# First attention stage: the causal penalty preset in the scores' banks, and P's transposes placed right behind the scores

## The chip, the cores and the metric

The kernel runs on one core of a Trainium2 chip. The metric is the device time of one execution in microseconds (us). It is a single launch that computes two blocks of a small transformer on an input of 4 sequences of 512 tokens with 128 features each, all in 32-bit floats.

## The reference, cut to what matters

The whole is `x = x + attention(layernorm(x))`, then `x = x + six local attention and feed-forward layers(layernorm(x))`. The change lies in the first half alone. That half is an ordinary causal attention with 16 heads of 64 features, whose mask is not minus infinity but a finite penalty of -50:

```python
q = (x @ Wq).reshape(b, s, HEADS, HEAD_DIM)      # k and v alike
scores = SCALE * jnp.einsum('bqhd,bkhd->bhqk', q, k)
causal = jnp.triu(jnp.ones((s, s), dtype=x.dtype), k=1)
scores = scores + MASK_PENALTY * causal
attn = jax.nn.softmax(scores, axis=-1)
out = jnp.einsum('bhqk,bkhd->bqhd', attn, v).reshape(b, s, HEADS * HEAD_DIM)
return out @ Wr
```

Because the penalty is finite, all keys count for every query, and all 512 columns of the scores are computed.

## The kernel before, in words

The order of the work is written out by hand: each engine executes its instructions in the order in which the program issues them, and semaphores tell an engine that something it reads is there, or that a buffer it writes is free.

**Slots.** The first stage has 64 slots, numbered m = 0 to 63. There are 4 sequences (`b`), 8 pairs of heads each (`c`), and 4 row tiles of 128 queries each (`t`). A slot does two row tiles of one pair of heads: an even slot tiles 0 and 1, an odd slot tiles 2 and 3. An object of the class `Rows` is one row tile; `now` are the two of this slot, `old` the two of the slot before.

**What a row tile goes through.**

- `scores` (line 308): q times k for both heads into `ps_sc`, two banks of PSUM, 512 columns per head. The two heads lie in the two halves of the array's rows and run side by side. 4 products of 256 columns; a 32-bit product is 2 instructions of TensorE, so a row tile is 8 records.
- `penalty` (line 323): for each head, one 16-bit product of an identity with the 128x128 triangle `pen` adds -50 above the diagonal in the tile's own block of columns. The blocks to the right of it get their -50 through a second bias (line 339) of the exponents.
- `maximum` (VectorE, line 335): the row maxima of both heads, over 1024 columns.
- `exponents` (ScalarE, line 348): 4 instructions: for each head the seen columns, and for each head the columns right of them with the other bias. The last tile has 2, of 512 columns. Each also sums its row into `den`.
- `inverse` (VectorE, lines 358 and 359), `normalise` (GpSimd, line 362): the exponents times 1/`den`.
- `transposes` (TensorE, line 373), one slot later: 4 transposes per head into a bank `ps_pt`. ScalarE copies head 0's bank to SBUF (line 377), VectorE head 1's (line 381). There are two such banks, so each group of 4 transposes waits until the group two before it has been copied out.
- `times_v1` (line 393), four slots later, 4 products of 512 columns per slot; after the second half VectorE copies the result out (line 403).

**What else is in a slot.** An even slot projects the next pair's q (line 271, copied by ScalarE, line 273), an odd one its k (line 277, copied by VectorE, line 279). Odd slots also project a part of v (line 287, copied by ScalarE, line 294; the first two slots two parts more), but for the last four odd slots of the last sequence. All these go through one single bank `ps_pj`: the next product into it waits for the copy of the one before. Some even slots hold a step of a layernorm, in the same bank: a mean (line 109, then VectorE line 111 and a square on ScalarE, line 113), a variance (line 118, then an inverse root of 12 small GpSimd instructions, lines 81 to 84), and a scaling (line 126, then VectorE line 130). The odd slots with c = 1 of the later three sequences end with the output projection of the sequence before (line 407, 8 products of 512 columns), again in that bank.

**The order in a slot, before.** TensorE: `times_v1`, scores of both tiles, penalties of both tiles, v or a layernorm step, transposes of `old[0]`, q or k, transposes of `old[1]`, output projection. ScalarE: v's copy or the square, head 0's copy of `old[0]`, the exponents of `now[0]`, those of `now[1]`, q's copy, head 0's copy of `old[1]`. VectorE: the copy of line 403, a scaling step, the maximum of `now[0]`, mean or variance, bias, head 1's copy of `old[0]`, maximum and bias of `now[1]`, k's copy, `inverse` of `now[0]`, head 1's copy of `old[1]`, `inverse` of `now[1]`.

After the first stage come the six local layers with their own loop of slots; their code is unchanged.

Of the kernel before, what the change touches and what calls it, by code (L numbers as in the profile page):

```python
# [8 lines left out]
F32 = mybir.dt.float32  # L9
# [6 lines left out]
P = 128  # L16
# [16 lines left out]
def body(ctx: ExitStack, tc: tile.TileContext, a, out: bass.AP):  # L33
# [156 lines left out]
    with tc.manual_schedule():  # L190
# [2 lines left out]
        wv = s1.tile([P, INNER], F32, tag="wv", name="wv")  # L193
        wr = s1c.tile([P, NC, EMB], F32, tag="wr", name="wr")
        pen = s1.tile([P, P], BF16, tag="pen", name="pen")
        xr = [s1.tile([P, NT, EMB], F32, tag="xr", name=f"xr{b}", bufs=2) for b in range(B)]
        for b in range(B):
            src = x[b].rearrange("(t p) e -> p t e", p=P)
            if b:
                nc.sync.dma_start(out=xr[b], in_=src)  # L200
            else:
                nc.sync.dma_start(out=xr[b][:, 0:2], in_=src[:, 0:2])
                nc.scalar.dma_start(out=xr[b][:, 2:NT], in_=src[:, 2:NT])
                nc.sync.dma_start(out=ident16, in_=a["ident16"])
                nc.sync.dma_start(out=pen, in_=a["pen"])
        for t_, n_ in ((wq, "wq"), (wk, "wk"), (wv, "wv")):
            nc.scalar.dma_start(out=t_, in_=a[n_])
        nc.sync.dma_start(out=wr, in_=a["wr"].rearrange("(c p) e -> p c e", p=P))
# [87 lines left out]
        class Rows:  # L296


            def __init__(self, b, c, t):
                self.b, self.c, self.t = b, c, t  # L300

            def scores(self):
                b, c, t = self.b, self.c, self.t
                sc = self.sc = ps1.tile([P, 2, S], F32, tag="sc", name="ps_sc", bufs=2)
                for k0 in range(0, S, S // 2):
                    for h in range(2):
                        rows = slice(h * HD, (h + 1) * HD)
                        mm(  # L308
                            sc[:, h, k0 : k0 + S // 2],
                            lhsT=qs[b, c][rows, t * P : (t + 1) * P],  # L310
                            rhs=ks[b, c][rows, k0 : k0 + S // 2],
                            start=(k0 == 0),
                            stop=False,
                            skip_group_check=True,
                        )

# [24 lines left out]
            def exponents(self):  # L341
                self.pr = s1.tile([P, 2, S], F32, tag="pr1", name="pr1", bufs=3)
                self.den = small.tile([P, 2, 2], F32, tag="den", name="den")
                seen = (self.t + 1) * P
                for part_, cols in enumerate((slice(0, seen), slice(seen, S))):
                    for h in range(2):
                        if cols.start < S:
                            nc.scalar.activation(  # L348
                                self.pr[:, h, cols],
                                self.sc[:, h, cols],  # L350
                                AF.Exp,
                                bias=self.nm[:, part_, h : h + 1],
                                accum_out=self.den[:, part_, h : h + 1],
                            )

            def inverse(self):
                if self.t + 1 < NT:
# [26 lines left out]
        def times_v1(b, c, half):  # L384

            if half == 0:
                os_[b, c] = ps1b.tile([P, S], F32, tag="o1", name="ps_o1", bufs=1)
            o = os_[b, c]
            for k in (2 * half, 2 * half + 1):
                for h in range(2):  # L390
                    col = (2 * c + h) % HEADS * HD
                    j, col = col // 512, col % 512
                    mm(  # L393
                        o[h * HD : (h + 1) * HD, :],
                        lhsT=vs[b, j][:, k, col : col + HD],
                        rhs=pTs[b, c][:, h, k, :],
                        start=(k == 0),
                        stop=(k == NT - 1),
                        skip_group_check=True,
                    )  # L400
# [21 lines left out]
        for m in range(last):  # L422
# [2 lines left out]
            old = rows[2 * m - 2 : 2 * m] if m else []  # L425
            if m >= 4:
                g = m // 2 - 2
                times_v1(g // NC, g % NC, odd)
# [7 lines left out]
            scale = None  # L436
            if not odd and c == 3 and b + 1 < B:
                scale = norms[b + 1][2]
            if b in range(1, B) and not odd and c == 6:
                scale = norms1[b - 1][2]  # L440
            if scale:
                scale()
# [9 lines left out]
            if not odd and 1 <= c <= 2 and b + 1 < B:  # L452
                if c == 1:
                    norms[b + 1] = norm_x(b + 1)
                norms[b + 1][c - 1]()
            if b in range(1, B) and not odd and 4 <= c <= 5:
                norms1[b - 1][c - 4]()
            if now:
                now[0].bias()
# [21 lines left out]
            if now:  # L481
                now[1].exponents()
            for f in copies:
                f()
            if now:
                now[1].inverse()
                now[1].normalise()
            if out_:
# [399 lines left out]
    def first_slot():  # L888
# [8 lines left out]
        rows[-1].transposes(later=True)()  # L897
        first_step()
        square(new, 0)
        times_v1(B - 1, NC - 2, 1)  # L900
        rotate(new, 0)
        sum_squares(new, 0)
        add_rotated(new, 0)
# [8 lines left out]
        times_v1(B - 1, NC - 1, 1)  # L912
        second_step()
        over_norm(new, 0)
        over_norm(new, 1)
# [188 lines left out]
def _constants(n):  # L1104
# [42 lines left out]
    return {"tabs": tabs, "band": band, "pen": pen, "ident16": ident16, "zeros": zeros}  # L1147


# [49 lines left out]
```

## Time and profile before

| | |
|---|---|
| time, median of 3 runs (lowest, highest) | 2072.2 us (2071.69, 2074.13) |
| the profiled execution's own time | 2072.4 us |
| its span | 2070.6 us |
| mean granted TensorE clock | 0.996 |
| first scores start / last slot's scores start | 23.5 us / 523.2 us |
| busy in 130 to 200 us: TensorE, VectorE, ScalarE, GpSimd | 69.99, 46.58, 43.67, 32.76 of 70 us |

The span is what the profiler saw between the first and the last instruction; the rest of the execution's time, 1.8 us, lies around it. "PE" is TensorE's products, "PEld" its loads of weights, DVE is VectorE, ACT ScalarE, POOL GpSimd, SP the queue that issues most transfers. A line of the timeline gives start, length, engine, source line, operation, what it writes from what, and in brackets how long the engine had been idle and what ended that. The chain of waits walks back from the last instruction to whatever released each one; its pieces are lengths of time that add up.

### The profile page before, as it was taken

Reading aid. Unit: us, or ns where it says so; the run is one execution under the profiler, and the core shown is the slowest. Engines: PE = TensorE matmul, PEld = TensorE weight load, DVE = VectorE, ACT = ScalarE, POOL = GpSimd, SP = SyncE. Lnnn points to the kernel's source line nnn. Section 1 sums busy time; section 2 is a strip of 40 time slices with the busy share of each in tenths; the row PEclk is TensorE's granted clock in tenths of the full one; section 3 lists DMA queues with packets and bytes.
Section 4 is the critical chain, followed back from the end, with each engine's and each line's share of the span. In section 5 each row is a group of like instructions: output and inputs, shape, how many; then the busy total and the mean of one; then the engine's idle time right before and its main releaser. Section 6 shows DMA issues by size and latency. Waiting matters only on the chain.

```text
span 2070.6 us, 77263 instructions
## 1 busy us (share of the span) xinstructions
PE 2028.4 (98%) x34382; PEld 1329.1 (64%) x34382; DVE 1640.8 (79%) x2240; ACT 1368.2 (66%) x2678; POOL 1316.5 (64%) x1432
## 2 busy tenths in 40 slices
PE   7999999999999999999999999999999999999998
PEld 5665555655466666666666666666666666666665
DVE  3766766767698888888888888888888888888885
ACT  3665665666455766676776676776667776677763
POOL 1554554555677677667767667667677767667762
PEclk8999999999999999999999999999999999999999
DMA  3000000000011121111211112111121111211110
GB/s 127 1 1 1 1 1 1 1 1 1 12 44 36 42 67 44 44 44 33 77 44 34 54 36 64 53 35 44 46 64 44 38 51 46 67 41 44 38 45 27
DMA packets 34968, 77.44 MB, mean 37 GB/s; under 512 B 4686, under 2 KB 18764, under 8 KB 34636
## 3 DMA queue, kind: packets, MB, share of 16 engines
q1 hardware_dynamic: 33932, 70.79, 11.8%
q8 instruction: 272, 4.46, 0.9%
q10 hardware_dynamic: 704, 1.70, 0.2%
q14 instruction: 60, 0.49, 0.1%
HBM read 23.50 MB, written 1.05 MB: 12 GB/s over the span
## 4 chain that ended last, share of the span: by engine, by line
PE 91%; DVE 5%; ACT 2%; POOL 1%; issue 1%; DMA 0%; SPq 0%; POOLq 0%; ACTq 0%
PE ps_proj L548 23%; PE ps_one L661 12%; PE ps_one L762 7%; PE ps_att L737 7%; PE ps_sc L308 6%; PE ps_o L393 6%; PE ps_att L700 5%; PE ps_pt L373 5%; PE ps_proj L812 3%; PE ps_proj L813 3%; PE ps_proj L832 3%; PE ps_pj L287 1%; PE ps_att L690 1%; PE ps_pj L277 1%; PE ps_pj L271 1%; PE ps_pj L407 1%
## 5 line engine op out<-in xcount | busy, mean ns | idle before, releaser
L587 POOL TENSOR_TENSOR rot<-rot,t 128x1024 f32<-128x1024 f32 x192 | 454.2, 2366 | 232.6 <-DVE t L576 220.1
L548 PE MATMUL ps_proj<-wqkv,xs 128*128 128x512 f32 x1152 | 569.0, 602 | 0.5 <-PE ps_one L661 0.2
L362 POOL TENSOR_TENSOR pr<-pr,den 128x1024 f32<-128x1024 f32 x128 | 241.0, 1893 | 248.3 <-DVE den L359 238.5
L606 POOL TENSOR_TENSOR rot<-rot,ss 128x1024 f32<-128x1024 f32 x192 | 361.3, 1903 | 7.4
L560 ACT ACTIVATE sq<-ps_proj 128x1024 f32<-128x1024 f32 x192 | 196.4, 1023 | 93.8 <-PE ps_proj L548 93.6
L548 PEld LDWEIGHTS ps_proj<-wqkv,xs 128*128 128x128 f32 x1152 | 188.2, 190 | 102.0 <-issue 92.1
L570 DVE TENSOR_TENSOR rot<-ps_proj,lt 128x1024 f32<-128x1024 f32 x192 | 233.3, 1215 | 10.2 <-ACT sq L560 10.0
L576 DVE TENSOR_TENSOR t<-ps_proj,lt 128x1024 f32<-128x1024 f32 x192 | 232.9, 1213 | 0.0
L348 ACT ACTIVATE pr<-ps_sc,nm 128x128 f32<-128x128 f32 (+3 forms) x448 | 220.3, 509 | 11.8 <-DVE nm L335 8.6
L565 DVE TENSOR_REDUCE ss<-sq 128x16 f32<-128x1024 f32 x192 | 221.1, 1190 | 0.0
L661 PEld LDWEIGHTS ps_one<-ident,rot 128*128 128x128 f32 x1536 | 172.7, 141 | 61.2 <-issue 51.2
L661 PE MATMUL ps_one<-ident,rot 128*128 128x128 f32 x1536 | 205.1, 276 | 1.1 <-POOL xs L170 0.6
L335 DVE TENSOR_REDUCE nm<-ps_sc 128x2 f32<-128x1024 f32 x128 | 155.9, 1218 | 62.9 <-PE ps_sc L323 62.8
L664 ACT COPY pT<-ps_one 128x512 f32<-128x512 f32 x192 | 110.0, 587 | 136.6 <-PE ps_one L661 136.6
L762 PEld LDWEIGHTS ps_one<-aT,wo 128*128 128x128 f32 x1536 | 182.9, 192 | 23.6 <-issue 17.7
L762 PE MATMUL ps_one<-aT,wo 128*128 128x128 f32 x1536 | 189.1, 276 | 0.3 <-ACT tmp_t L852 0.2
L746 DVE RECIPROCAL rden<-ps_att 128x8 f32<-128x8 f32 x192 | 38.8, 202 | 176.8 <-PE ps_att L737 176.7
L648 ACT COPY vt<-ps_proj 128x512 f32<-128x512 f32 x192 | 103.1, 590 | 96.4 <-PE ps_proj L548 96.4
L373 PEld LDWEIGHTS ps_pt<-ident,pr 128*128 128x128 f32 x1024 | 117.4, 142 | 58.5 <-issue 47.4
L664 ACT COPY qT<-ps_one 128x512 f32<-128x512 f32 x192 | 103.1, 589 | 66.1 <-PE ps_one L661 66.1
L377 ACT COPY pT<-ps_pt 128x512 f32<-128x512 f32 x128 | 75.6, 591 | 98.0 <-PE ps_pt L373 98.0
L373 PE MATMUL ps_pt<-ident,pr 128*128 128x128 f32 x1024 | 135.9, 274 | 3.0 <-DVE pT L381 2.4
(178 smaller groups left out, 3763.2 us busy)
## 6 DMA issues: line engine op xcount, KB each, us to landing
vs<-vt SPq DMA_DIRECT2D x96, 390.0 KB, 3.7
vs<-vt SPq DMA_DIRECT2D x72, 130.0 KB, 3.6
wqkv<-in_wqkv_dram SPq DMA_DIRECT2D x18, 512.0 KB, 4.0
vs<-in_zeros_dram SPq DMA_DIRECT2D x24, 130.0 KB, 3.7
wo<-in_wo_dram SPq DMA_DIRECT2D x6, 512.0 KB, 4.2
w<-in_w_dram SPq DMA_DIRECT2D x6, 341.0 KB, 5.9
xr<-in_x_dram SPq DMA_DIRECT2D x3, 256.0 KB, 7.6
scales<-in_scales_dram SPq DMA_DIRECT2D x6, 128.0 KB, 3.1
```

What stands on the lines that cost most here:

```text
L348: nc.scalar.activation(self.pr[:, h, cols], self.sc[:, h, cols], AF.Exp, bias=self.nm[:, part_, h : h + 1], accum_out=self.den[:, part_, h ...
L362: nc.gpsimd.tensor_tensor(self.pr, self.pr, self.den[:, 0].unsqueeze(2).to_broadcast([P, 2, S]), ALU.mult)
L373: nc.tensor.transpose(pt[:, k * P : (k + 1) * P], self.pr[:, h, k * P : (k + 1) * P], ident)
L548: mm(p[:, c, :], lhsT=u.xs[:, u.T * P : (u.T + 1) * P], rhs=wpart[j][:, c * 512 : (c + 1) * 512], start=True, stop=True,)
L565: nc.vector.tensor_reduce(u.ss[:, j * HEADS : (j + 1) * HEADS], heads(u.sq[j]), AX.X, ALU.add)
L570: nc.vector.tensor_tensor(heads(t0), heads(pf), lt[:, u.T, 2 * j].unsqueeze(1).to_broadcast([P, HEADS, HD]), ALU.mult)
L576: nc.vector.tensor_tensor(t1.rearrange("p (h t d) -> p h t d", t=2, d=half), pf.rearrange("p (h t d) -> p h t d", t=2, d=half)[:, :, ::-1, :],
L587: nc.gpsimd.tensor_tensor(u.r[j], u.r[j], u.t1, ALU.add)
L606: nc.gpsimd.tensor_tensor(heads(u.r[j]), heads(u.r[j]), u.ss[:, j * HEADS : (j + 1) * HEADS].unsqueeze(2).to_broadcast([P, HEADS, HD]), AL ...
L661: nc.tensor.transpose(tp[:, c * P : (c + 1) * P], src[:, (4 * g + c) * P : (4 * g + c + 1) * P], ident)
L664: nc.scalar.copy(dst[:, 4 * g : 4 * g + 4, col0 : col0 + P], tp.rearrange("p (c t) -> p c t", c=4))
L762: mm(y[:, 0:P], lhsT=wo_w[0][:, k, :], rhs=u.aT[:, g].rearrange("p (j f) -> p j f", f=P)[:, :, f0 : f0 + W], start=(k == 0), stop=(k == NC ...
```

## The change

The penalty products are left out in all slots but the first. In their place ScalarE copies a 32-bit triangle `pen32` (one more small input) for both heads into the tile's own block of `ps_sc`, before the scores, and the scores are added to it. For that the scores of a head are cut into three products: the own block of 128 columns (added to what stands there), the far pair of blocks with 256 columns, and the neighbour block with 128. The preset for the same bank in the next slot stands on ScalarE behind the last exponents that read the bank.

The order in a slot is another one too. TensorE: `times_v1`, scores, transposes of `old[0]`, v or a layernorm step, transposes of `old[1]`, q or k, output projection. ScalarE: head 0's copy of `old[0]`, the seen exponents of `now[0]`, v's copy or the square, the other exponents of `now[0]`, the preset for the next slot's first tile, the exponents of `now[1]`, the preset for its second tile, head 0's copy of `old[1]`, q's copy. VectorE: maximum and bias of `now[0]`, the copy of line 403, head 1's copy of `old[0]`, the layernorm steps (scaling now in the same place as the others), maximum and bias of `now[1]`, head 1's copy of `old[1]`, k's copy, both `inverse`.

```diff
+        pen32 = s1.tile([P, P], F32, tag="pen32", name="pen32")
...
                 nc.sync.dma_start(out=pen, in_=a["pen"])
+                nc.sync.dma_start(out=pen32, in_=a["pen32"])
...
+            def preset(self):
+                sc = self.sc = ps1.tile([P, 2, S], F32, tag="sc", name="ps_sc", bufs=2)
+                nc.scalar.copy(
+                    sc[:, :, self.t * P : (self.t + 1) * P], pen32.unsqueeze(1).to_broadcast([P, 2, P])
+                )
...
             def scores(self):
                 b, c, t = self.b, self.c, self.t
-                sc = self.sc = ps1.tile([P, 2, S], F32, tag="sc", name="ps_sc", bufs=2)
-                for k0 in range(0, S, S // 2):
+                own = self.sc is not None
+                if not own:
+                    self.sc = ps1.tile([P, 2, S], F32, tag="sc", name="ps_sc", bufs=2)
+                sc, far = self.sc, (1 - t // 2) * 2
+                for k, (k0, n) in enumerate(((t, 1), (far, 2), (t ^ 1, 1))):
+                    cols = slice(k0 * P, (k0 + n) * P)
                     for h in range(2):
                         rows = slice(h * HD, (h + 1) * HD)
                         mm(
-                            sc[:, h, k0 : k0 + S // 2],
+                            sc[:, h, cols],
                             lhsT=qs[b, c][rows, t * P : (t + 1) * P],
-                            rhs=ks[b, c][rows, k0 : k0 + S // 2],
-                            start=(k0 == 0),
-                            stop=False,
+                            rhs=ks[b, c][rows, cols],
+                            start=(k == own),
+                            stop=own or k == 2,
                             skip_group_check=True,
                         )
...
-                nc.vector.tensor_copy(at, o)
+                return lambda: nc.vector.tensor_copy(at, o)
...
             for r in now:
                 r.scores()
-            for r in now:
+            for r in now if m == 0 else ():
                 r.penalty()
...
-            if now:
-                now[0].maximum()
+            now[0].maximum()
+            now[0].bias()
+            if m >= 4:
+                keep()
+            if old:
+                old[0].transposes()
+            now[0].exponents((0,))
             if m < 2:
                 make_v(0, 0, 2 * m)
                 make_v(0, 0, 2 * m + 1)
...
-            if old:
-                old[0].transposes()
-            out_ = b > 0 and c == 1 and odd
-            if now:
-                now[0].exponents()
-                if not out_:
-                    now[1].maximum()
-                    now[1].bias()
+            now[0].exponents((1,))
+            if m + 1 < last:
+                rows[2 * m + 2].preset()
+            now[1].maximum()
+            now[1].bias()
+            copies = []
+            if old:
+                copies.append(old[1].transposes(later=True))
             bn, cn = (b, c + 1) if c + 1 < NC else (b + 1, 0)
-            copies = []
             if bn < B:
                 copies.append((make_k if odd else make_q)(bn, cn))
-            if out_ and now:
-                now[1].maximum()
-                now[1].bias()
-            if now:
-                now[0].inverse()
-                now[0].normalise()
-            if old:
-                copies.append(old[1].transposes(later=True))
-            if now:
-                now[1].exponents()
+            now[0].inverse()
+            now[0].normalise()
+            now[1].exponents()
+            if m + 1 < last:
+                rows[2 * m + 3].preset()
             for f in copies:
                 f()
```

More of the change, by code (lines that the diff above doesn't have):

```diff
@@ L299, in __init__ @@
             def __init__(self, b, c, t):
[L300 removed]
+                self.b, self.c, self.t, self.sc = b, c, t, None
+            def preset(self):
[3 more added lines that the diff above has]
+                )
             def scores(self):
                 b, c, t = self.b, self.c, self.t
[L304 to L305 removed]
+                own = self.sc is not None
[4 more added lines that the diff above has]
+                    cols = slice(k0 * P, (k0 + n) * P)
                     for h in range(2):
@@ L339, in bias, with exponents @@
                     nc.vector.tensor_scalar(self.nm[:, 1], self.nm[:, 0], PEN, None, ALU.add)
-            def exponents(self):
-                self.pr = s1.tile([P, 2, S], F32, tag="pr1", name="pr1", bufs=3)
-                self.den = small.tile([P, 2, 2], F32, tag="den", name="den")
+            def exponents(self, parts=(0, 1)):
+                if 0 in parts:
+                    self.start_exponents()
                 seen = (self.t + 1) * P
@@ L346, in exponents @@
                     for h in range(2):
-                        if cols.start < S:
+                        if part_ in parts and cols.start < S:
                             nc.scalar.activation(
@@ L354, in exponents, with start_exponents @@
                             )
+            def start_exponents(self):
+                self.pr = s1.tile([P, 2, S], F32, tag="pr1", name="pr1", bufs=3)
+                self.den = small.tile([P, 2, 2], F32, tag="den", name="den")
             def inverse(self):
@@ L402, in times_v1 @@
                 at = aTs[b, c] = s1c.tile([P, S], F32, tag="aT1", name="aT1", bufs=NC + 2)
-                nc.vector.tensor_copy(at, o)
+                return lambda: nc.vector.tensor_copy(at, o)
+            return lambda: None
         def project_out1(b, y):
@@ L427, in body @@
                 g = m // 2 - 2
-                times_v1(g // NC, g % NC, odd)
+                keep = times_v1(g // NC, g % NC, odd)
             for r in now:
                 r.scores()
-            for r in now:
+            for r in now if m == 0 else ():
                 r.penalty()
@@ L434, in body @@
                 load_x(m)
[L436 to L442, printed above, removed]
-            if now:
-                now[0].maximum()
+            now[0].maximum()
[5 more added lines that the diff above has]
+            now[0].exponents((0,))
             if m < 2:
@@ L451, in body @@
                 make_v(b + 1, 0, c - NT)
-            if not odd and 1 <= c <= 2 and b + 1 < B:
+            if not odd and 1 <= c <= 3 and b + 1 < B:
                 if c == 1:
@@ L455, in body @@
                 norms[b + 1][c - 1]()
-            if b in range(1, B) and not odd and 4 <= c <= 5:
+            if b in range(1, B) and not odd and 4 <= c <= 6:
                 norms1[b - 1][c - 4]()
-            if now:
-                now[0].bias()
-            if old:
-                old[0].transposes()
-            out_ = b > 0 and c == 1 and odd
-            if now:
-                now[0].exponents()
-                if not out_:
-                    now[1].maximum()
-                    now[1].bias()
+            now[0].exponents((1,))
[4 more added lines that the diff above has]
+            copies = []
+            if old:
+                copies.append(old[1].transposes(later=True))
             bn, cn = (b, c + 1) if c + 1 < NC else (b + 1, 0)
-            copies = []
             if bn < B:
                 copies.append((make_k if odd else make_q)(bn, cn))
-            if out_ and now:
-                now[1].maximum()
-                now[1].bias()
-            if now:
-                now[0].inverse()
-                now[0].normalise()
-            if old:
-                copies.append(old[1].transposes(later=True))
-            if now:
-                now[1].exponents()
+            now[0].inverse()
[3 more added lines that the diff above has]
+                rows[2 * m + 3].preset()
             for f in copies:
                 f()
[L485 to L488, printed above, removed]
+            now[1].inverse()
+            now[1].normalise()
+            if b > 0 and c == 1 and odd:
                 y = bank1()
@@ L899, in first_slot @@
         square(new, 0)
-        times_v1(B - 1, NC - 2, 1)
+        times_v1(B - 1, NC - 2, 1)()
         rotate(new, 0)
@@ L911, in first_slot @@
         inverse_norms(new)
-        times_v1(B - 1, NC - 1, 1)
+        times_v1(B - 1, NC - 1, 1)()
         second_step()
@@ L1146, in _constants @@
     zeros = np.zeros((W, 2, NC, HD + 1), f)
-    return {"tabs": tabs, "band": band, "pen": pen, "ident16": ident16, "zeros": zeros}
+    return {"tabs": tabs, "band": band, "pen": pen, "pen32": pen.astype(f), "ident16": ident16, "zeros": zeros}
 def kernel(**inputs):
```

## The prediction, made before the changed kernel had run

> **What bounds the kernel now.** I read the page's head first (engines, then the 40 slices), then the chain of waits in two neighbouring slots, then the timeline of a slot in which transposes already follow transposes.
>
> ```profile
> span 2070.6 us, 77263 instructions
> ...
> PE 2028.4 (98%) x34382; PEld 1329.1 (64%) x34382; DVE 1640.8 (79%) x2240; ACT 1368.2 (66%) x2678; POOL 1316.5 (64%) x1432
> ...
> PE   7999999999999999999999999999999999999998
> ...
> PEclk8999999999999999999999999999999999999999
> ```
>
> TensorE is busy nearly throughout, at full granted clock. The first stage is the first ten slices (scores start at 23.5 us, the last slot's at 523.2).
>
> ```profile
> by line: PE ps_sc L308 37.3%; PE ps_o L393 28.7%; PE ps_pt L373 22.5%; PE ps_pj L271 10.8%; PE ps_sc L323 4.1%
> ...
> 104.33 1.93 PE ps_sc L308 x16
> 106.25 0.33 PE ps_sc L323 x4
> 106.58 0.88 PE ps_pt L373 x8
> 107.46 0.86 PE ps_pj L271 x2
> 108.32 0.92 PE ps_pt L373 x8
> 109.24 1.87 PE ps_o L393 x8
> ```
>
> A plain even slot is TensorE work end to end, with no piece of another engine: 6.78 us from scores to scores. Odd slots add v's product and last 7.72. So whatever leaves TensorE's queue is gained, and whatever it must wait for is lost. Each tr (8 transposes, 0.87 us) now has 0.86 us of other work between it and the next: that is cover, and the change takes it away. What its loss costs is on view in slot 62, the next to last, where no q is left to project and the two groups of transposes follow each other:
>
> ```profile
> 518.57 1.04 PE L373 MATMUL ps_pt<-ident,pr 128*128 128x128 f32 x8
> 518.66 1.22 DVE L335 TENSOR_REDUCE nm<-ps_sc 128x2 f32<-128x1024 f32 x1 [1.80 <-PE ps_sc L323]
> 519.21 0.58 ACT L377 COPY pT<-ps_pt 128x512 f32<-128x512 f32 x1 [2.15 <-PE ps_pt L373]
> ...
> 519.94 0.63 PE L373 MATMUL ps_pt<-ident,pr 128*128 128x128 f32 x4 [0.33 <-POOL pr L362]
> ...
> 519.99 0.68 DVE L381 COPY pT<-ps_pt 128x512 f32<-128x512 f32 x1
> ```
>
> Each half of the second group waits until a copy has emptied its bank. The first half starts 0.15 us after ScalarE's copy ends (519.79), whatever the label names; the second begins at 520.73, 0.06 after VectorE's copy, and its first transpose lasts 0.055 longer than the others (its weights). The next product of another line begins at 521.32, 2.75 us after 518.57, where 16 transposes at 0.109 and a 0.13 change of tile shape make 1.87: 0.88 us lost.
>
> **The change, part by part.** Times count from the first score of a slot (s), and slots from 0.
>
> 1. *Penalties out.* From the first penalty to the next line's first product is 0.23 us (518.33 to 518.57). 63 slots: **-14.5**.
>
> 2. *Scores in three pieces.* The records of line 308 start 0.216 apart in pairs (two heads at once). Per slot 8 such pairs (1.72) become 4 of 256 columns and 8 of 128. A 128-column pair is bounded below by half, 0.108, and above by the pace of weight loads: line 118 (one column, so loads alone) starts 0.1115 apart, and the second head's load goes out 0.007 behind the first's: 0.119. I take 0.112, line 118's pace: 0.86 + 0.90 = 1.76, +0.034 in 64 slots: **+2.2** (0 to +6).
> [...]
>
> 3. *Transposes behind transposes.* The first group starts at s+1.96. Its head 0 is done after 4x0.109 + 0.165 (a transpose lasts 0.273 and the next starts after 0.109) = 0.60, ScalarE copies 0.04 later for 0.585, TensorE's first useful column comes 0.11 after (0.06 + 0.05): 1.34 instead of 0.87, 0.47 lost. Head 1 is done at 1.04; VectorE is free (the maximum now waits for the first tile alone: s+1.2 to 2.4), copies until 1.76, +0.11 = 1.87 against 1.78: 0.09 more. 0.56 per slot in the 12 even slots without a layernorm step and in slots 57 and 61, which have no v: +7.8. Slot 62 has it already and loses less than its 0.88: -0.35. **+7.5**.
>
> 4. *k waits for v's copy* (odd slots). v ends at s+3.70. On ScalarE the copy now stands behind head 0's copy (from s+2.60, the next may start 0.48 later) and two exponents of 384 columns (0.555 each, start to start): s+4.19 to 4.78. k's product goes at 4.89; the second transposes end at 4.57. 0.32 lost, less 0.04 that k's piece shows over q's now. 26 slots with v from slot 5 on: **+7.3**. Before, v's copy was first in the slot.
>
> 5. *Output projection directly behind k*, in the same single bank: k's copy must end first. What such a succession costs: line 287 behind line 287 starts 1.80 us apart at 35.90, for 0.86 of product, 0.94 lost; so far the second transposes covered it. 3 slots: **+2.7**.
>
> 6. *Layernorm steps* stand behind VectorE's copy now. Mean (5 slots): the square starts on ScalarE at s+4.6 and the queue behind it, 0.48 + 2x0.555 + 0.5 for a preset between exponents (their accumulators are read out first) + 4x0.45 + 0.6 to the second preset's end, is through at s+9.05, while the next slot's second tile, which needs that preset, is due at s+8.35: it starts 0.1 later still, 0.75 late after 0.16 today, +0.6 each; q's wait of 0.16 in these slots goes: +2.2. Variance (6 slots): 12 GpSimd operations at 0.285 (3.4 us) start at s+4.6 instead of about 4.0, `normalise` behind them ends at s+9.9, the next first transposes are due at 9.35: 0.75 with the hand-over, and 0.9 once more in slot 59 for the second: +5.4. Scaling (6 slots): bank waits that now cost about 0.7 (slot 22 lasts 7.93 against 6.78 + 0.44) fall to 0.25: -2.7. **+4.9**.
>
> 7. *Presets.* No copy of 128x256 by ScalarE into PSUM stands in the trace. Ends: 0.23 (line 598, 32 columns) and 0.68 (exponent of 512). Nearest: the copy of 512 takes 0.59, and 256 columns fewer are worth 0.20 (exponents 0.68 and 0.48): **0.39**. [...] In plain slots ScalarE's idle time hides two presets (43.67 of 70 us busy; the second ends at s+7.65, the next slot's second tile is due at s+8.0). In slots 0 to 3 TensorE waits for exponents today (the scores' two tiles start 1.82 apart at 31.02 and 32.84), so 8 presets are paid there: **+3.1**. From about 0.55 each on the cover in even slots is gone too. Ends: -2 and +12 us on the whole sum.
>
> 8. *The rest at nothing:* pen32's 64 KB on SP's queue ahead of the later sequences' x (0 to 0.3 us: the first 25 us move 262 GB/s, and x of sequence 1 is needed only in the first normalisation); VectorE and GpSimd do the same work.
>
> Sum: -14.5 + 2.2 + 7.5 + 7.3 + 2.7 + 4.9 + 3.1 = **+13.2**. The profiled execution took 2072.4 (span 2070.6 and 1.8 around it), 0.2 above the median: 2085.6, rounded **2086**.
>
> **Rivals.**
>
> - *The waits stay covered (faster).* TensorE is full, and 14.5 leaves its queue. If copies came early enough that the second transposes find both banks empty and k finds v's copy done, only parts 1, 2, 5 and 7 remain: 2072.4 - 6.5 = 2066. It decides at 0.10 us of new waiting per slot. Against it: two copies of 0.59 and 0.68 cannot fit behind 0.87 us of transposes even on idle engines; slot 62 shows it.
> - *Only the banks cost (no change).* If v's copy and the layernorm steps slip in without delay: parts 1, 2, 3, 5, 7: +1, 2073. For it: ScalarE is idle a third of the time. Against: v's copy is behind exponents in program order.
> - *ScalarE becomes the bound.* A preset of 0.6 to 0.68: +7 to +12 more, 2093 to 2098. For it: even slots have only 0.35 to spare; against: copies run shorter than exponents.
> - *The scores don't get by with less.* If the two heads' loads went one after the other, 128-column pairs would take 0.22: +55, about 2140. Against: the second pair of loads of a slot starts 0.108 behind the first pair, with both heads' products running.
>
> **How the numbers follow.** A difference under 0.2% (4 us) can't be told from none. Chances: forecast 0.68 (its own range 2078 to 2093), ScalarE bound 0.14, only the banks 0.10, covered 0.06, loads in series 0.02. Range 2076 to 2098: it takes in both ends of the preset (-2, +12) and leaves out the faster case and most of the unchanged one. Faster 0.06, the same 0.10, slower 0.84.
>
> **What would show it.** Right: plain even slots of about 7.1 us with an idle of TensorE before the second transposes ended by ScalarE's copy; odd ones of about 7.7 with a wait before k; about 13 us more than today between the first and the last slot's scores (499.7); scores plus hand-over 1.9 instead of 2.16. Wrong: no wait before the second group of transposes; the second tile's scores waiting for presets in plain slots (ScalarE); 128-column records more than 0.12 apart in pairs.

## The result and the profile after

The changed kernel took **2093.9 us** (median of 4 runs, 2092.3 to 2095.2) where the kernel before took 2073.2 beside it (4 runs, 2071.7 to 2076.0): ratio 1.0103, 95% interval 1.0090 to 1.0116, so 1% slower. The prediction was 2086 in a range of 2076 to 2098. The sign came out as predicted, and so did most of the forecast waits; the loss of 21 us is over half as large again as the forecast 13, because of two things for which the prediction has no term. The profiled execution took 2095.2 us.

The head of the page of the kernel after, engines and slices:

```profile
span 2093.5 us, 77885 instructions
...
PE 2030.4 (97%) x34642; PEld 1332.7 (64%) x34642; DVE 1676.2 (80%) x2240; ACT 1418.7 (68%) x2804; POOL 1318.4 (63%) x1432
...
PE   7999999999999999999999999999999999999997
...
PEclk7999999999999999999999999999999999999999
```

TensorE does no less: the span is 22.9 us longer at nearly the same busy time. ScalarE gained 50.5 us, 47.4 of them the presets. VectorE gained 35.4 us, although the change gives it nothing to do. No term of the prediction has that last number; it is the lead to what was missed.

The chain of waits through a plain even slot after (slot 10), the counterpart of the slot shown for before; columns are start, length, what:

```profile
111.77 1.96 PE ps_sc L322 x24
113.73 0.60 PE ps_pt L391 x4
114.33 0.02 issue
114.35 0.59 ACT pT L395
114.95 0.14 issue
115.08 1.11 PE ps_pt L391 x8
116.19 0.86 PE ps_pj L273 x2
117.05 1.87 PE ps_o L411 x8
```

Where before had only TensorE, ScalarE's copy of head 0's bank now stands on the chain between the two groups of transposes, as predicted: 0.33 us of idle TensorE, and a slot of 7.15 us instead of 6.78. The last slot but one, which had its transposes back to back before too, shows the milder form of the same wait; the timeline of TensorE there:

```profile
541.47 1.10 PE L391 MATMUL ps_pt<-ident,pr 128*128 128x128 f32 x8
542.90 1.11 PE L391 MATMUL ps_pt<-ident,pr 128*128 128x128 f32 x8 [0.33 <-ACT pT L395]
```

Before, the second group waited there for ScalarE and then again for VectorE. Now the maximum starts as soon as the first tile's scores are there, VectorE is done sooner, and only the first wait is left.

The lengths of all slots, sorted by what a slot holds, give the account. Sums of (after - before) in us, the forecast by the prediction's terms beside them, and in the last column a kernel of the experiments (e5):

| slots | count | forecast | after | e5 |
|---|---|---|---|---|
| 0 to 3 | 4 | +2.5 | +5.9 | +6.9 |
| plain even | 12 | +4.4 | +4.4 | +4.2 |
| plain odd | 11 | +0.9 | +1.7 | +1.1 |
| mean, and the odd slots after it (without projection) | 5 + 3 | +0.6 | +0.9 | +0.5 |
| odd slots with the output projection | 3 | +4.2 | +4.0 | +4.0 |
| variance | 6 | -1.2 | -1.2 | -1.2 |
| odd slots after a variance | 6 | +5.6 | **+6.9** | **+3.0** |
| scaling | 6 | -3.9 | -3.5 | -3.5 |
| odd slots after a scaling | 6 | +0.8 | **+3.8** | **+0.9** |
| 62 | 1 | -0.5 | -0.5 | -0.5 |
| 4 to 62 together | 59 | +10.8 | +16.5 | +8.5 |

Two places do not fit: the odd slots behind layernorm steps, and the start.

**VectorE's longer time.** The groups of instructions by line; after the bar total busy us and the mean of one in ns, then the idle time before them. The bias (a scalar added to 128x2) and the addition of the two parts of the denominator (128x2 plus 128x2), before:

```profile
L358 DVE TENSOR_TENSOR den<-den 128x2 f32<-128x2 f32 x96 | 30.9, 322 | 40.2 <-ACT pr L348 39.7
L339 DVE TENSOR_SCALAR nm<-nm 128x2 f32<-128x2 f32 x96 | 18.7, 195 | 2.9
```

and after:

```profile
L353 DVE TENSOR_SCALAR nm<-nm 128x2 f32<-128x2 f32 x96 | 58.9, 614 | 3.3
L376 DVE TENSOR_TENSOR den<-den 128x2 f32<-128x2 f32 x96 | 27.6, 287 | 48.4 <-ACT pr L362 48.4
```

The same 96 biases cost 40 us more. What they wait for is seen in slot 9, VectorE's timeline and then GpSimd's:

```profile
104.79 1.23 DVE L349 TENSOR_REDUCE nm<-ps_sc 128x2 f32<-128x1024 f32 x1
106.05 1.10 DVE L353 TENSOR_SCALAR nm<-nm 128x2 f32<-128x2 f32 x1
107.06 0.68 DVE L421 COPY aT<-ps_o 128x512 f32<-128x512 f32 x1
107.66 0.67 DVE L399 COPY pT<-ps_pt 128x512 f32<-128x512 f32 x1
```

```profile
105.23 1.90 POOL L380 TENSOR_TENSOR pr<-pr,den 128x1024 f32<-128x1024 f32 x1 [0.74 <-ACT q L275]
```

The bias, 2 numbers in each partition, lasts 1.10 us and ends at 107.15, 0.02 after GpSimd's normalisation (107.13). That is no accident. Counted over the trace: of the 96 biases after, 60 start while a normalisation runs, all 60 last over 0.25 us, and all 60 end within 0.035 us of a normalisation's end; the other 36 take 0.17. Before, 16 were of that kind. The addition does the same (33 before, up to 1.09 us; 21 after, up to 1.67); in each kernel one of these ends with another multiplication of GpSimd and the others with a normalisation. The maximum (1.20 to 1.23 us), the reciprocal (0.15 to 0.17) and the copies out of PSUM (0.67 to 0.69) show nothing of it. I call this *holding*. By starting the maximum earlier the change moved the bias of the first tile into the normalisation of the row before. Behind it in VectorE's queue stand the copy of line 421, head 1's bank and the second maximum; in slot 9 TensorE's second group of transposes waits 0.45 us for that bank.

The plain odd slots have nearly the forecast length (7.82 for 7.80), but in the changed kernel not for the forecast reason. The chain of waits through slot 11 (window 118 to 128 us):

```profile
118.92 1.10 PE ps_sc L322 x12
...
120.04 1.24 DVE nm L349
...
121.30 0.74 DVE nm L353
122.04 0.59 DVE aT L421
122.63 0.61 DVE pT L399
...
123.29 0.66 PE ps_pt L391 x4
123.94 0.94 PE ps_pj L279 x2
```

TensorE waits for head 1's bank, behind the held bias, and k's product then follows the transposes at once; v's copy has ended 0.08 us before it. With the holding taken away (e5, below) the chain in the same slot does go through v's copy (window 117 to 128 us):

```profile
123.03 0.48 ACT v L299
...
123.56 1.13 PE ps_pj L282 x2
```

That slot takes 7.82 as well: the two waits hide each other, and that they come out alike is chance.

The traces show holding for the scalar addition (up to 1.66 us, after) and for the two-input addition (up to 1.67), and none for the reduction (the maximum, at most 1.23). Why these two and not the reduction, no run shows. The normalisation does not last longer for it: 1.90 us at most, before and after alike.

**The start.** TensorE's granted clock, in stretches of the profile (length, busy PE, PEld, DVE, ACT, POOL, then PEclk, DMA share, GB/s), before:

```profile
20.30:23.70 3.40, 2.52 (x6) 0.83 (x6) 0.69 (x1) 0.60 (x1) 0.00 (x0) 0.74 0.43 150
23.70:27.10 3.40, 3.01 (x22) 1.85 (x20) 1.34 (x3) 0.35 (x1) 0.00 (x0) 1.00 0.00 0
```

and after:

```profile
20.30:23.70 3.40, 2.52 (x5) 0.46 (x4) 0.69 (x1) 0.60 (x1) 0.00 (x0) 0.50 0.41 138
23.70:27.10 3.40, 3.40 (x24) 3.19 (x24) 0.00 (x0) 0.00 (x0) 0.00 (x0) 0.50 0.03 5
27.10:30.50 3.40, 2.19 (x11) 0.99 (x9) 2.61 (x4) 1.28 (x5) 0.00 (x0) 0.80 0.00 0
```

The first scores ran at half clock in this execution (full from 28.5 us instead of 22.25, and half once more from 42.25 to 45.5; such times are read in steps of 0.25 us).

### The profile page after: what moved, and what is told of

Read it like the earlier page. It is cut to its first block, busy times and chain, and to the rows that moved or that the text cites. A ratio compares the mean times of both kernels' runs of the same rounds, so it can differ in the third digit from the quotient of the medians.

```text
span 2093.5 us, 77885 instructions
## 1 busy us (share of the span) xinstructions
PE 2030.4 (97%) x34642; PEld 1332.7 (64%) x34642; DVE 1676.2 (80%) x2240; ACT 1418.7 (68%) x2804; POOL 1318.4 (63%) x1432
## 3 DMA queue, kind: packets, MB, share of 16 engines
HBM read 23.57 MB, written 1.05 MB: 12 GB/s over the span
## 4 chain that ended last, share of the span: by engine, by line
PE 84%; DVE 9%; ACT 4%; POOL 1%; issue 1%; DMA 0%; SPq 0%; POOLq 0%; DVEq 0%; ACTq 0%
PE ps_proj L555 23%; PE ps_one L668 12%; PE ps_one L769 7%; PE ps_att L744 7%; PE ps_att L707 5%; PE ps_o L411 4%; PE ps_sc L322 4%; PE ps_pt L391 4%; PE ps_proj L819 3%; PE ps_proj L820 3%; PE ps_proj L839 3%; ACT pr L362 2%; DVE nm L349 2%; PE ps_att L697 1%; DVE nm L353 1%; PE ps_pj L279 1%
## 5 line engine op out<-in xcount | busy, mean ns | idle before, releaser
L391 PE MATMUL ps_pt<-ident,pr 128*128 128x128 f32 x1024 | 145.7, 281 | 17.1 <-DVE pT L399 7.5
L322 PEld LDWEIGHTS ps_sc<-k,q 64*128 64x128 f32 x1536 | 114.0, 189 | 67.8 <-ACT ps_sc L308 37.7
L391 PEld LDWEIGHTS ps_pt<-ident,pr 128*128 128x128 f32 x1024 | 112.4, 142 | 58.7 <-POOL pr L380 23.8
```

Of the source, the lines that this page charges most:

```text
L322: mm(sc[:, h, cols], lhsT=qs[b, c][rows, t * P : (t + 1) * P], rhs=ks[b, c][rows, cols], start=(k == own), stop=own or k == 2, skip_group_ ...
L391: nc.tensor.transpose(pt[:, k * P : (k + 1) * P], self.pr[:, h, k * P : (k + 1) * P], ident)
```

## The experiments

The theory they were to test: the order costs as forecast, holding comes on top, the preset itself is cheap. Its rivals: the presets on ScalarE are what costs; the waits move elsewhere when one is removed.

### Holding taken away: e3, e5

e3 computes the bias on ScalarE.

```diff
-                    nc.vector.tensor_scalar(self.nm[:, 1], self.nm[:, 0], PEN, None, ALU.add)
+                    nc.scalar.activation(self.nm[:, 1], self.nm[:, 0], AF.Identity, bias=minus50)
```

> The changed kernel with the bias (128x2, the maximum plus the penalty) computed on ScalarE instead of VectorE. Theory (a small VectorE instruction on SBUF that starts while GpSimd normalises ends only when GpSimd does, and the copy, the second bank and TensorE's transposes wait behind it): VectorE loses some 40 us of such waiting, TensorE's waits fall by about 6: 2094 - 6 = 2088, a plain even slot 7.15 -> about 7.05 and slot 9 more. Rival (the long bias is off the path, and the layernorm steps and banks alone make the loss): no change or slower by ScalarE's 96 added instructions, 2094 to 2098.

It took 2090.0 us, ratio 1.0095 (1.0081 to 1.0108); slots 4 to 62 fell by 2.7 us (478.3 against 481.0), not 6. The slots after a scaling lost what was expected (+0.9 instead of +3.8), slot 9 came back to 7.82. But the slots after a variance grew (+7.5 instead of +6.9), probably because 96 instructions of 0.30 us joined ScalarE's queue, and plain even slots stayed at 7.15: holding is no part of their wait. The price of holding could not be read from this run, so the next one leaves the work on VectorE.

e5 writes bias and addition as reductions over two elements, in the same places.

```diff
-                    nc.vector.tensor_scalar(self.nm[:, 1], self.nm[:, 0], PEN, None, ALU.add)
+                    nc.vector.tensor_reduce(
+                        self.nm[:, 1], self.nm[:, 0::2].rearrange("p k h -> p h k"), AX.X, ALU.add
+                    )
...
-                    nc.vector.tensor_tensor(self.den[:, 0], self.den[:, 0], self.den[:, 1], ALU.add)
+                    nc.vector.tensor_reduce(den, self.den[:, 0:2].rearrange("p k h -> p h k"), AX.X, ALU.add)
```

(The row 2 of each `nm` holds the constant -50; `den` here is a third row.)

> The changed kernel with VectorE's bias and its addition of the two parts of the denominator written as reductions over two elements, at the same places on the same engine, SBUF to SBUF as before. Theory (VectorE's scalar addition and its addition of two SBUF inputs are held until GpSimd's normalisation ends, a reduction is not): bias and addition take under 0.25 us wherever they start; VectorE's busy time falls by some 55 us; the slots after the scaling steps (7, 23, 29, 39, 45, 61) fall by 0.3 to 1.0 as they did with the bias on ScalarE, slots 9, 49 and 54 by 0.2 to 0.3, and slots 59, 21 and 57 by 0.2 to 0.4: 4 to 5 us less than the changed kernel run beside it. Rival (reductions are held as well, or the holding is off the path): no change.

The same groups of e5:

```profile
L357 DVE TENSOR_REDUCE nm<-nm 128x2 f32<-128x4 f32 x96 | 15.1, 157 | 3.3
L384 DVE TENSOR_REDUCE den<-den 128x2 f32<-128x4 f32 x96 | 14.5, 151 | 49.1 <-ACT pr L368 46.8 <-ACT ps_sc L311 2.3
```

60 of these biases and 26 of these additions start while a normalisation runs, and none lasts over 0.16 us. The time: **2086.3 us** (2085.0 to 2087.9), ratio 1.0071 (1.0059 to 1.0084), against 2094.3 for the unchanged changed kernel beside it (e8, 1.0110, 1.0096 to 1.0124): 8.0 us less, and slots 4 to 62 are 7.9 us shorter than e8's. That is more than the 4 to 5 expected: what was expected to fall fell, and the slots after a variance fell by 3.9 together, where 0.2 to 0.4 had been expected in two of them. So holding costs 8 us, nearly all in odd slots and mostly behind layernorm steps; the table's last column is the change without it.

### The order without the preset: e2

The changed order, but penalties as products and scores in two pieces:

```diff
-            for r in now if m == 0 else ():
+            for r in now:
                 r.penalty()
...
-            if m + 1 < last:
-                rows[2 * m + 2].preset()
...
```

> The changed kernel's order, but with the penalties as products and the scores in two pieces, so without presets. If the terms of the prediction are right and nothing else is at work: 2072.4 + 7.5 + 7.3 + 2.7 + 4.9 = 2095. Theory (besides, GpSimd's normalisation holds up VectorE's bias, and TensorE waits about 6 us for what stands behind it): up to 2101; less if the 0.33 us of the penalties move the bias back out of the normalisation. Rival (the order costs little, the loss is the preset's): 2072 to 2080.

It took **2113.0 us**, ratio 1.0203 (1.0189 to 1.0217), above both numbers: the order alone costs 43 us, of which the preset gives 19 to 21 back, more than the 12 of penalties and pieces. Why is seen in a plain even slot that begins at 96.78, VectorE and then TensorE:

```profile
99.03 1.23 DVE L345 TENSOR_REDUCE nm<-ps_sc 128x2 f32<-128x1024 f32 x1 [2.70 <-PE ps_sc L333]
100.29 0.17 DVE L349 TENSOR_SCALAR nm<-nm 128x2 f32<-128x2 f32 x1
100.37 0.68 DVE L395 COPY pT<-ps_pt 128x512 f32<-128x512 f32 x1
```

```profile
98.94 1.04 PE L387 MATMUL ps_pt<-ident,pr 128*128 128x128 f32 x8
100.32 0.63 PE L387 MATMUL ps_pt<-ident,pr 128*128 128x128 f32 x4 [0.33 <-ACT pT L391]
101.11 0.66 PE L387 MATMUL ps_pt<-ident,pr 128*128 128x128 f32 x4 [0.17 <-DVE pT L395]
```

The maximum waits for the penalties, which stand behind both tiles' scores, 1.05 us later in the slot than after (2.25 instead of 1.20); so head 1's copy is late as well and TensorE waits twice; a plain even slot is 0.86 us longer than before. That is the 0.88 that the prediction read from slot 62, now in every such slot. The preset helps this order because the first tile's maximum no longer waits for the second tile.

### q between the transposes again: e4, e6

```diff
+            if bn < B and not odd:
+                copies.append(make_q(bn, cn))
             if old:
                 copies.append(old[1].transposes(later=True))
-            if bn < B:
-                copies.append((make_k if odd else make_q)(bn, cn))
+            if bn < B and odd:
+                copies.append(make_k(bn, cn))
```

> The changed kernel with q's product between the two groups of transposes again in even slots (k stays behind them in odd slots). Prediction's part 3 (0.56 us lost per even slot without cover, 12 plain even slots): the even slots fall back by 0.37 to 0.56, sum -6 to -8, so 2086 to 2088, plain even slots 6.6 to 6.8. Rival (the copies are late for another reason, so q's product only moves the wait to the next bank): under 2 us gained, 2092 to 2094.

It took 2100.2 us, ratio 1.0145 (1.0131 to 1.0159): **slower** by 6 (medians) to 9 us (ratios) than the changed kernel, outside both expectations. Yet the plain even slots came to 6.58, 0.57 below 7.15: the prediction's 0.56 per slot. The odd slots gave it back (8.32 instead of 7.82). VectorE there, from the end of an even slot on:

```profile
87.37 1.85 DVE L376 TENSOR_TENSOR den<-den 128x2 f32<-128x2 f32 x1 [0.23 <-ACT pr L362]
89.25 0.17 DVE L377 RECIPROCAL den<-den 128x2 f32<-128x2 f32 x1
89.33 1.20 DVE L349 TENSOR_REDUCE nm<-ps_sc 128x2 f32<-128x1024 f32 x1
90.57 0.93 DVE L353 TENSOR_SCALAR nm<-nm 128x2 f32<-128x2 f32 x1
```

Holding strikes twice in a row: the addition starts 0.06 us after a normalisation and is held for 1.85 us, and the bias for 0.93. e6 is the same with e5's reductions:

> The edit of the run before with q's product between the two groups of transposes in even slots as well. There, with the holding, even slots lost nothing (6.58) but odd slots took 8.32 instead of 7.82. Theory (the odd slots' loss there is the holding: the addition of the denominator lasted 1.85 us and the bias 0.93 us ahead of the maximum and the copies): odd slots return to about 7.8, even ones stay at 6.6, and the whole is 10 to 14 us below the changed kernel. Rival (the odd slots wait because VectorE's and ScalarE's copies are late whatever the holding): odd slots stay at 8.2 to 8.3, and at most 5 us is gained.

2089.3 us, ratio 1.0085 (1.0071 to 1.0099): 11 us below e4, but 3 *above* e5. Odd plain slots take 8.17, and it is another wait now. TensorE in e6:

```profile
101.82 2.37 PE L325 MATMUL ps_sc<-k,q 64*128 64x128 f32 x24
104.12 1.09 PE L399 MATMUL ps_pt<-ident,pr 128*128 128x128 f32 x8
```

The 24 records of the scores take 2.37 instead of 2.03: the second tile's stop for its preset, which ScalarE ends at 102.99 behind its last exponents. The prediction gave an even slot 0.35 us to spare on ScalarE; a slot shorter by 0.57 has used that up. And where an even slot holds a layernorm step, q between adds a third product in the one bank, with less between them: 8.49 instead of 7.61 (mean), 8.22 instead of 7.35 (scaling), 7.89 instead of 7.43 (variance). Both expectations were half right: without holding the odd slots fall, but ScalarE comes next.

### v's copy first: e11

e5 with v's product and copy issued ahead of the first tile's exponents:

```diff
-            now[0].exponents((0,))
             if m < 2:
...
             elif odd and b + 1 < B:
                 make_v(b + 1, 0, c - NT)
+            now[0].exponents((0,))
```

> The kernel of e5 (changed order, nothing held) with v's product and its copy issued ahead of the first tile's exponents on ScalarE. Prediction's part 4 (k waits 0.32 us for v's copy in odd slots): odd plain slots 7.82 to about 7.5, 26 slots, 2086 - 8 = 2078. Rival (the exponents that now stand behind v's copy start 1.1 us later, and the presets and normalisations with them): odd slots or the even ones after them grow by as much or more, 2086 or above.

2086.2 us, ratio 1.0066 (1.0053 to 1.0079): no difference from e5 that can be measured. The odd plain slots did fall, 7.82 to 7.51, the prediction's 0.28 to 0.32. The even plain slots after them rose from 7.15 to 7.37; TensorE in one:

```profile
105.81 2.25 PE L325 MATMUL ps_sc<-k,q 64*128 64x128 f32 x24
107.99 1.09 PE L399 MATMUL ps_pt<-ident,pr 128*128 128x128 f32 x8
109.41 1.11 PE L399 MATMUL ps_pt<-ident,pr 128*128 128x128 f32 x8 [0.33 <-ACT pT L403]
```

Again the scores' group is stretched (2.25 instead of 2.03): the exponents that now come later delay the second tile's preset, which ends at 106.86, and that tile's scores start at 106.91 instead of 106.79. In this trace slots 4 to 62 are 2.7 us shorter than in e5, of 8 that the copy itself saves.

### The preset in the old order: e1, e7, e9, e10

e1 is the kernel before with preset and three pieces:

```diff
                 now[1].exponents()
+                if m + 1 < last:
+                    rows[2 * m + 3].preset()
```

(and the first tile's preset likewise behind `now[0].exponents()`).

> The order of the kernel before, with the preset and the scores in three pieces (the preset of the next slot's first tile stands behind the first exponents, that of the second tile behind the second). Theory (the order is what costs, the preset and the three pieces are cheap): 2072.4 - 14.5 (penalties out) + 2.2 (pieces) + 3 (slots 0 to 3, where ScalarE is on the path) = 2063; a plain even slot 6.78 - 0.20 = 6.58, a plain odd one 7.52. Rival (ScalarE's presets delay what TensorE waits for, whatever the order): 2072 or more, with TensorE waiting for a preset or for a copy of ScalarE in plain slots. About 3 us more than the sum would come back if the granted clock stays at half as long at the start as in the changed kernel (to 29 us rather than 23).

2080.5 us, ratio 1.0046 (1.0030 to 1.0061): the rival, though of these 9 to 11 us only 2.3 lie in slots 4 to 62 of the profile and 3.7 in slots 0 to 3. Even plain slots took the forecast 6.58 (-0.20), odd ones 7.89 (+0.17, 0.37 more than the sum). TensorE and ScalarE at the turn to an odd slot:

```profile
100.80 2.36 PE L322 MATMUL ps_sc<-k,q 64*128 64x128 f32 x24
103.09 1.12 PE L289 MATMUL ps_pj<-wv,xnT 128*128 128x512 f32 x2
```

```profile
100.99 0.48 ACT L362 ACTIVATE pr<-ps_sc,nm 128x256 f32<-128x256 f32 x1
101.34 0.21 ACT L362 ACTIVATION_READ_ACCUMULATOR pr<-ps_sc,nm 128x1 f32 x1
101.59 0.38 ACT L308 COPY ps_sc<-pen 128x256 f32<-128x256 f32 x1
```

The second tile's scores are due half way through the group, at 100.80 + 0.98 = 101.78. The last sums of the exponents are read out by 101.55, so the bank alone would be free in time; the preset behind them ends at 101.97. The second tile starts at 102.02, the group takes 2.36 us instead of 2.03, and the slot is the 0.37 longer. The old order had 0.23 us to spare there, and the preset needs 0.38 and its hand-over. So e7 presets the first tile alone, where the bank is free half a slot earlier; the second tile keeps its penalty products. Against e1:

```diff
-                if m + 1 < last:
-                    rows[2 * m + 3].preset()
```

> The order of the kernel before, with the preset for the first tile of a slot alone; the second tile keeps its penalty products and its scores in two pieces. With both presets in that order the odd plain slots took 7.89 instead of 7.52, because the second tile's preset stands between the second exponents and the scores that need it. Theory (that preset alone is on the path, the first one is covered): even and odd plain slots both 0.23/2 - 0.02 = 0.10 shorter than before (6.68 and 7.62), the whole 4 to 6 us below before. Rival (any preset delays ScalarE's queue and so the copies): odd slots stay above 7.7, the whole at or above before.

All plain slots fell as expected, 6.64 and 7.62, and slots 4 to 62 by 4.0 us (460.4 against 464.4). But the time stayed: 2072.1 us, ratio 1.0003 (0.9994 to 1.0012), with slots 0 to 3 at 39.8 instead of 35.3. Against e7, e9 presets only from slot 4 on:

```diff
-                if m + 1 < last:
+                if 4 <= m + 1 < last:
                     rows[2 * m + 2].preset()
```

> The kernel with the old order and the preset for the first tile alone, but with presets only from slot 4 on (slots 0 to 3 keep the penalty products). With presets from slot 1 its slots 4 to 62 were 5 us shorter than before and its slots 0 to 3 were 4.5 us longer. Theory (the presets at the start cost, as ScalarE is on the path there): slots 0 to 3 as before (35.3), 2072 - 5 = 2067, ratio 0.9975. Rival (the start is longer because TensorE's clock stays at half for some more microseconds in most executions of any kernel): slots 0 to 3 at 37 to 40 again when the profile's clock rises at 28 us, ratio about 1.000.

2071.7 us, ratio 0.9999 (0.9990 to 1.0008), not the 2067 of the theory. Its slots 1 to 3 are as before to 0.01 us, and slot 0 is 1.96 longer with the clock at full only from 27.5 us; slots 4 to 62 are 3.9 us shorter. And e10, that with e5's reductions:

> The run before plus the bias and the addition of the denominator as reductions. In the kernel before 16 of 96 biases and some additions were held by GpSimd, mostly in slots with layernorm steps. Theory (holding costs only where something is queued behind it on TensorE's path; the old order has cover): 0 to 2 us less than the run before. Rival (holding costs as much as in the changed order): 6 to 8 us less, 2060.

2071.1 us, ratio 0.9995 (0.9987 to 1.0004), 4.2 us shorter in slots 4 to 62: holding (43 biases in e9) costs 0.3 us of slot time in an order that has cover, as expected. Neither is a measurable gain over before.

### The start: e8, e12

e8 is the changed kernel unaltered.

> The changed kernel once more, beside the others of this call. Ratio 1.010 as before. [...]

2094.3 us, ratio 1.0110. Full clock came at 29.25 us, and there was a half-clock stretch from 56.5 to 60. Over all profiles of kernels with `pen32` it came at 20.75 (e11), 22.75, 23.25, 24.0, and nine times between 27.5 and 29.25: it differs between executions. With early full clock and no later half stretch (e3, e11) slots 0 to 3 took 38.3 us, +3.0; in the changed kernel's two profiles 41.2 and 41.0.

But chance alone it is not. The mean granted clock was read in every execution, not only in the profiled ones: 0.9957 for the kernel before (45 executions, 0.994 to 0.997), and between 0.9926 and 0.9942 for each of the kernels with `pen32` (0.9942 and 0.9938 for the changed kernel, 4 executions each). 0.0015 to 0.0019 of 2070 us is an estimated 3 to 4 us of clock. A straight line through all executions of e1 to e12 and of before, with one level for each kernel and each session of runs, gives 1.0 us of time for 0.001 of clock; by that the changed kernel's share is 1.5 to 2 us. What brings the lower clock is open. In e9 slots 0 to 3 have the order of before and no preset of their own, and its clock came late all the same (27.5) and averages 0.9939; no run adds the one more input alone.

e12 is e5 with presets from slot 4 on only.

> The kernel of e5 with presets only from slot 4 on; slots 0 to 3 keep penalty products and scores in two pieces. Prediction's part 7 (8 presets on the path at the start, 3.1 us, less 0.8 for penalties and pieces): slots 0 to 3 some 2.3 us shorter where the clock rises at the same time, 2084. Rival (the order and the clock make the start long, not the presets): slots 0 to 3 as in e5, 2086 to 2087.

2083.1 us (2082.4 to 2084.9), ratio 1.0057 (1.0044 to 1.0069): 3.1 us below e5 by the medians, measured beside other runs of before, so by the ratios 3 with about as much uncertainty. An estimated 1.4 of it is the clock (0.9926 for e5, 0.9940 for e12). Pairs whose clock ran alike through slots 0 to 3 show the presets' price better. The changed kernel and e2, which has none (both at half until 28.5 and again from 42.25 to 45.5), took 41.2 and 40.2 us there; e1 and e9 (both at half until 27.5) 39.0 and 37.2. So the presets cost 1.0 us there in the changed order and 1.8 in the old one, net of the penalties and pieces; the prediction's terms make 2.5. The new order costs something there by itself: slots 2 and 3 of e2 and e12, without presets, take 7.53 and 9.52 instead of 7.39 and 9.06.

## Why the prediction was right in sign and too small

- **Part 1 and 2** (-14.5, +2.2): right. Slots in which nothing else changed, the even plain ones of e1, are 0.20 shorter, the forecast 0.196.
- **Part 3** (+7.5): right. 0.37 net per plain even slot against 0.364 forecast; with q put back, 0.57 against 0.56.
- **Part 4** (+7.3): right in size once nothing is held: in e5 0.10 net per plain odd slot against 0.084, and moving v's copy forward gave 0.31. In the changed kernel itself the wait before k, one of the prediction's signs of being right, does not show: another wait of nearly the same length stands before it. (The sign's "about 7.7" is not what the terms add up to, 7.72 - 0.20 + 0.28 = 7.80.)
- **Part 5** (+2.7): right; the three slots took 4.0 more together, 4.2 forecast with the mean's share.
- **Part 6** (+4.9): the mean and scaling terms hold (even slots -1.5 and -3.5 against -1.8 and -3.9). The variance term was too large: without holding, the six odd slots after it cost 3.0 and not 5.6.
- **Part 7** (+3.1): the preset took 0.376 us, the estimate 0.39. In slots 0 to 3 it cost 1.0 to 1.8 net, not 2.5. That these slots grew by 3.0 at early full clock, close to the sum, is luck: the order's own cost there had no term.
- **Part 8** (nothing) is the step that failed. "VectorE and GpSimd do the same work" is true of the amount and not of the moment. The cost of a VectorE instruction depended on what GpSimd was doing: the biases alone took 40 us more of VectorE's time, and all holding together cost 8.0 us at the end (e5 against e8). What holding cost in the kernel before no run took away; in the nearest one, e9, it was 0.3. The sign of it was in the trace of before: 16 biases and 32 additions that lasted until a normalisation's end, in means of 0.195 and 0.322 us for instructions whose others take 0.17 and 0.16. I read the means and not the spread.

The account in the profiled execution: forecast 13.4 (the 13.2 without slot 63's -0.2), -2.3 for what slots 4 to 62 cost less without holding, +8.0 holding, +0.4 at the start, +2.9 there at half clock: 22.4, the measured growth from first to last scores (499.7 to 522.1). The medians are 20.8 and 22.1 apart; by the granted clocks above an estimated 1.5 to 4 us of that is the clock's, the second thing without a term.

That the time fell inside the range is partly luck. The range reached to 2098 for a preset as dear as 0.6 us or more; the preset cost 0.376, and holding and the clock took up that room.

Of the rivals, ScalarE was no bound in the changed order (no plain slot of after waits for a preset; the five slots behind a mean do, as part 6 has it), but e6 and e11 show it next in line: a slot shorter by 0.57, or one whose exponents come later, runs into the second tile's preset.

Settled in part: why e9 and e10, 4 us shorter in the slots, are not shorter as a whole. Stretches of half clock fall in different places of their profiles (775 to 781 us in e9, for one), as they do in before's (2029 to 2032). Over 11 executions each their clock averages 0.9939 and 0.9942, against 0.9956 in the 21 of before beside them: by the line above an estimated 1.4 to 1.7 us of the 4. The rest is open.

## What to carry to other kernels

Moving an instruction can change its price: here the bias went from a mean of 195 ns to 614 because 60 of 96 instead of 16 were held by a multiplication of GpSimd. So before an order is changed, look at the spread of each small instruction, not its mean, and at what runs beside it where it lands. The scalar addition of 128x2 from SBUF to SBUF, 0.17 us alone, lasted until GpSimd's 1.90 us ended in all 60 cases of after, with all that was queued behind it; a reduction in its place took 0.16 at most (e5). And replacing products by a copy on another engine cost more than it saved where that copy stood between the last reader of the buffer and its next writer without time to spare (e1, ratio 1.0046); where it had time to spare (e7, e9), the slots became 4 us shorter, though the whole not measurably.

## What the runs showed of the hardware that was not expected

- VectorE's scalar addition and two-input addition of 128x2 in SBUF, 0.17 and 0.16 us alone, lasted up to 1.66 (after) and 1.85 us (e4) under GpSimd's 1.89 us multiplication; a reduction over two elements (0.16 at most), a reciprocal (0.17) and copies out of PSUM (0.69) did not lengthen.
- TensorE's granted clock came to full as late as 29.25 us after the start (e8; 20.75 in e11), although TensorE was busy 3.40 of 3.40 us in some stretches (in after from 23.7 to 27.1 us, at a clock of 0.50). It fell to half again later for 3.4 to 10.2 us (e8, at 2050 us), in e9 at 775 us after a stretch in which TensorE was busy 1.55 of 3.20 us, in e7 at 1278 after one of 1.72 of 3.40. What sets these times no run shows; the rise alone differs by 8.5 us between the executions here.
